# Slots of four samples instead of two in a streaming matmul with residual

## The chip, the cores and the metric

The kernel runs on one core of one Trainium2 chip. The metric is the device time of one execution in microseconds (us). The kernel before takes 327.6 us, the median of three runs (327.56 to 327.68).

## The reference

There are 128 samples, each a matrix of 128 channels by 1024 time steps in float32 (512 KB). Each sample has a subject number from 0 to 7, which picks one of eight 128 by 128 weight matrices. The output is the sample plus the product of its weights and itself:

```python
def reference(x, itok_B_0_7, L0_cond_weights):
    ...
        w = weights[subjects]
        out = jnp.einsum('bct,bcd->bdt', x, w)
        return out
    x = x + _L0_cond_ref(x, itok_B_0_7, L0_cond_weights)
    return x
```

So 67.1 MB are read, 67.1 MB are written, and between the two stand 128 products of a 128x128 matrix with a 128x1024 matrix.

## The kernel before, in words

The samples stay in SBUF in slots. A slot holds `G` = 2 samples side by side: in each of the 128 partitions (one for each channel) it has 2 x 1024 values, 8 KB without a gap. There are `SLOTS` = 23 slots, thus room for 46 samples, and `NT` = 128 / 2 = 64 turns of the loops over slots. Turn `i` uses slot `i % SLOTS`. The sum is written back over the sample in the slot, and the slot is stored from there.

Each engine has its own program, written out by hand in the order in which it runs; semaphores tie them together.

- SP issues the loads (L114 to L124), one DMA of 512 KB for each sample. From the second use of a slot on, it first waits until the store of the slot's last content has landed (L117). The load reads the sample in HBM as 32 runs of 16 KB (`ROWS` = 4 rows of 4 KB); each run goes to four partitions.
- POOL copies the weights of a sample's subject from `w_all`, which holds all eight matrices, into one of four small buffers (L142). It waits first for the load of `w_all` (L126), and for each sample until the product of four samples ago is done (L141).
- PE waits once for each slot until all loads of the slot have landed (L129), then for each sample for its weights (L144) and a free PSUM buffer (L146), and does two matmuls of 512 columns (L148). The profile shows each as two instructions, so there are four for a sample.
- DVE adds product and sample into the slot (L158), one instruction for each sample.
- ACT waits until all samples of the slot are added (L161) and issues one store for the whole slot, 1 MB (L162 to L167). From SBUF it reads one run for each partition, 8 KB; in HBM these go to two rows of 4 KB in two samples.
- At the end SP waits for the stores of the last `SLOTS` turns (L170, L171).

Loads and stores are issued through the function `transfer`, so that the profile puts both under L49. They use two DMA queues: q1 is SP's with the loads, q10 is ACT's with the stores, the load of `w_all` and that of the subject numbers. Each DMA ends with 16 writes of a semaphore, one for each DMA engine that took part.

Of the kernel before, what the change touches and what calls it, by code (L numbers as in the profile page):

```python
# [1 line left out]

# [4 lines left out]

F32 = mybir.dt.float32
I32 = mybir.dt.int32
ALU = mybir.AluOpType


G = 2

N = 512  # L30

SLOTS = 23

W_SLOTS = 4
P_SLOTS = 4
DMA = 16

ROWS = 4
QUEUES = {mybir.EngineType.SP: "qSPDynamicHW", mybir.EngineType.Activation: "qActDynamicHW"}


def transfer(nc, engine, out, in_):

    later, nc._always_lower_symbolic_ap = nc._always_lower_symbolic_ap, False
    ins, outs = engine.lower_ap_dma(in_), engine.lower_ap_dma(out)
    nc._always_lower_symbolic_ap = later
    return engine.add_instruction(  # L49
        mybir.InstDMACopy(  # L50
            name=nc.get_next_instruction_name(),
            engine=engine.engine,
            ins=ins,
            outs=outs,
            mode="Copy",
            cce_op=ALU.bypass,
            queue=QUEUES[engine.engine],
        )
    )


@with_exitstack
def kernel(
    ctx: ExitStack,
    tc: tile.TileContext,
    x: bass.AP,
    subjects: bass.AP,
    weights: bass.AP,
    out: bass.AP,
):  # L70
    nc = tc.nc
    B, C, T = x.shape
    S, _, D = weights.shape
    NT = B // G

    def sbuf(name, *shape, dtype=F32):
        return ctx.enter_context(nc.sbuf_tensor(name, list(shape), dtype)).ap()

    given, near, wrap, index = (
        sbuf(name, 1, B, dtype=I32) for name in ("given", "near", "wrap", "index")  # L80
    )
    w_all = sbuf("w_all", C, S, D)
    ws = [sbuf(f"w{i}", C, 1, D) for i in range(W_SLOTS)]
    xs = [sbuf(f"x{i}", C, G, T) for i in range(SLOTS)]
    ps = [
        ctx.enter_context(nc.psum_tensor(f"ps{i}", [D, T], F32)).ap() for i in range(P_SLOTS)
    ]

    s_given = tc.alloc_semaphore("s_given")
    s_wall = tc.alloc_semaphore("s_wall")  # L90
    s_index = tc.alloc_semaphore("s_index")
    s_copied = tc.alloc_semaphore("s_copied")
    s_product = tc.alloc_semaphore("s_product")
    s_added = tc.alloc_semaphore("s_added")
    s_load = [tc.alloc_semaphore(f"s_load{i}") for i in range(SLOTS)]
    s_store = [tc.alloc_semaphore(f"s_store{i}") for i in range(SLOTS)]

    with tc.tile_critical():  # L98

        nc.scalar.dma_start(given, subjects.rearrange("(o b) -> o b", o=1)).then_inc(s_given, DMA)  # L100
        nc.scalar.dma_start(w_all, weights.rearrange("s c d -> c s d")).then_inc(s_wall, DMA)

        nc.vector.wait_ge(s_given, DMA)
        nc.vector.tensor_scalar(near, given, -S, S - 1, ALU.max, ALU.min).then_inc(s_index, 1)  # L106
        nc.vector.wait_ge(s_index, 1)
        nc.vector.tensor_scalar(wrap, near, 0, S, ALU.is_lt, ALU.mult).then_inc(s_index, 1)  # L108
        nc.vector.wait_ge(s_index, 2)
        nc.vector.tensor_tensor(index, near, wrap, ALU.add).then_inc(s_index, 1)  # L110
        nc.gpsimd.wait_ge(s_index, 3)


        for i in range(NT):  # L114
            k, turn = i % SLOTS, i // SLOTS
            if turn:
                nc.sync.wait_ge(s_store[k], DMA * turn)  # L117
            for g in range(G):
                transfer(
                    nc,  # L120
                    nc.sync,
                    xs[k][:, g, :],
                    x[i * G + g].rearrange("(a r) t -> a (r t)", r=ROWS),
                ).then_inc(s_load[k], DMA)  # L124

        nc.gpsimd.wait_ge(s_wall, DMA)  # L126
        for i in range(NT):
            k, turn = i % SLOTS, i // SLOTS
            nc.tensor.wait_ge(s_load[k], DMA * G * (turn + 1))  # L129
            for g in range(G):  # L130
                b = i * G + g
                s = nc.values_load(  # L132
                    index[0:1, b : b + 1],
                    engines=[mybir.EngineType.Pool],
                    min_val=0,
                    max_val=S - 1,
                    skip_runtime_bounds_check_because="the index is clamped on the chip above",
                )
                w, p = ws[b % W_SLOTS], ps[b % P_SLOTS]
                if b >= W_SLOTS:  # L140
                    nc.gpsimd.wait_ge(s_product, b - W_SLOTS + 1)  # L141
                nc.gpsimd.tensor_copy(w, w_all[:, bass.ds(s, 1), :]).then_inc(s_copied, 1)  # L142

                nc.tensor.wait_ge(s_copied, b + 1)  # L144
                if b >= P_SLOTS:
                    nc.tensor.wait_ge(s_added, b - P_SLOTS + 1)  # L146
                for t in range(0, T, N):
                    mm = nc.tensor.matmul(  # L148
                        p[:, t : t + N],
                        w[:, 0, :],  # L150
                        xs[k][:, g, t : t + N],
                        start=True,
                        stop=True,
                    )
                mm.then_inc(s_product, 1)

                nc.vector.wait_ge(s_product, b + 1)
                nc.vector.tensor_tensor(xs[k][:, g, :], p, xs[k][:, g, :], ALU.add).then_inc(  # L158
                    s_added, 1
                )  # L160
            nc.scalar.wait_ge(s_added, (i + 1) * G)  # L161
            transfer(  # L162
                nc,
                nc.scalar,
                out[i * G : (i + 1) * G].rearrange("g d t -> d g t"),
                xs[k].rearrange("d (o g) t -> d o (g t)", o=1),
            ).then_inc(s_store[k], DMA)  # L167


        for i in range(NT - SLOTS, NT):  # L170
            nc.sync.wait_ge(s_store[i % SLOTS], DMA * (i // SLOTS + 1))  # L171


# [1 line left out]
_INS = ["x", "itok_B_0_7", "L0_cond_weights"]  # L175
_OUTS = [((128, 128, 1024), "float32")]


# [20 lines left out]
```

## Time and profile before

| what | value |
|---|---|
| median of three runs | 327.6 us |
| the profiled execution | 328.1 us |
| its span, first to last instruction | 326.3 us |
| PE busy | 237.0 us (73%) |
| DVE busy | 157.5 us (48%) |
| POOL busy | 37.8 us (12%) |
| DMA moved | 134.86 MB, mean 413 GB/s over the span |
| a matmul of 512 columns, mean | 616 ns, 592 ns at full clock |
| an add of one sample | 1225 ns |
| a load, issue to landing, median | 21.4 us |
| a store, issue to landing, median | 42.2 us |

The profile is of one execution. Its slices cut the span into 40 equal parts of 8.2 us; a digit is a busy share in tenths. For each DMA queue the page gives packets, MB and the time that the packets took, as a share of the time of 16 DMA engines. The same table can be had for a window of the span. A wait is told as "who waited <- for what: us in total, times, longest us". The chain of work is followed back from the last instruction, and its lines give start, duration and what ran. SPq and ACTq are the instruction queues of SP and ACT, which issue DMAs. PEclk is the clock that TensorE was granted, in tenths.

### The profile page before, as it was taken

What the parts mean: (1) busy time and instruction counts of PE and PEld (TensorE: products, weight loads), DVE (VectorE), ACT (ScalarE), POOL (GpSimd) and SP (SyncE); (2) the same over time, 40 slices, a digit from 0 to 9 for tenths busy, and PEclk for the clock granted to TensorE, in tenths of its full rate; (3) what the DMA queues carried; (4) which work ended last, traced back from release to release, by engine and by line L of the source; (5) the groups of instructions that cost most, each with busy time, mean ns of one, the idle gap of its engine ahead of it and who ended that gap; (6) DMA issues with size and microseconds to landing.
All of it is one profiled execution on the core that took longest, in us unless ns stands there. A gap on an engine that the chain in (4) does not pass through costs nothing.

```text
span 326.3 us, 1928 instructions
## 1 busy us (share of the span) xinstructions
PE 237.0 (73%) x512; PEld 97.1 (30%) x512; DVE 157.5 (48%) x131; POOL 37.8 (12%) x132
## 2 busy tenths in 40 slices
PE   0499999999999888999989887775979877000000
PEld 0144444444443333333333332231433332000000
DVE  0067766776677556556566554545445536000000
POOL 0111111111111111111111111111111100000000
PEclk9999999999999999999999999999798979755555
DMA  7999999999999999999999999999999999999993
GB/s 268 407 416 422 420 425 419 425 426 423 429 425 421 427 422 428 419 427 424 419 426 420 428 422 434 417 429 423 425 429 426 427 420 425 427 426 427 428 424 164
DMA packets 16411, 134.86 MB, mean 413 GB/s; under 512 B 3089, under 2 KB 4114, under 8 KB 4114
## 3 DMA queue, kind: packets, MB, share of 16 engines
q10 hardware_dynamic: 10258, 67.64, 49.6%
q1 hardware_dynamic: 6144, 67.12, 49.1%
q8 instruction: 4, 0.07, 0.1%
q14 instruction: 5, 0.04, 0.0%
HBM read 67.63 MB, written 67.11 MB: 413 GB/s over the span
## 4 chain that ended last, share of the span: by engine, by line
DMA 37%; another core or an unknown queue 22%; PE 17%; SPq 7%; DVE 1%; issue 1%; POOLq 0%; ACTq 0%; POOL 0%
DMA out_dram<-x 29%; PE ps L148 17%; SPq L49 7%; DMA x<-in_x_dram 5%; DMA w_all<-in_L_cond_weights_dram 3%; DVE x L158 1%; POOLq L132 0%; ACTq L100 0%; POOLq L142 0%; ACTq L195 0%; POOL w L142 0%; POOLq L126 0%; SPq L98 0%
## 5 line engine op out<-in xcount | busy, mean ns | idle before, releaser
L148 PE MATMUL ps<-x,w 128*128 128x512 f32 x512 | 237.0, 616 | 38.8 <-DMA x<-in_x_dram 26.2
L158 DVE TENSOR_TENSOR x<-ps,x 128x1024 f32<-128x1024 f32 x128 | 156.8, 1225 | 117.3 <-PE ps L148 117.3
L148 PEld LDWEIGHTS ps<-x,w 128*128 128x128 f32 x512 | 97.1, 195 | 177.8 <-issue 122.4
L142 POOL COPY w<-w_all 128x128 f32 x128 | 37.6, 294 | 230.6 <-PE ps L148 218.4
L106 DVE TENSOR_SCALAR near<-given 1x128 int32<-1x128 int32 x1 | 0.2, 215 | 2.2 <-DMA given<-in_itok_B_dram 2.2
L110 DVE CUSTOM_DVE_ANT_0 index<-near,wrap 1x256 uint16<-1x256 uint16 x1 | 0.3, 280 | 0.0
L108 DVE TENSOR_SCALAR wrap<-near 1x128 int32<-1x128 int32 x1 | 0.2, 216 | 0.0
L186 POOL MEMSET const-float32-0.0<- 128x1 f32 x1 | 0.1, 98 | 0.2 <-issue 0.2
L186 POOL MEMSET const-bfloat16-1.0<- 128x1 bf16 x1 | 0.1, 101 | 0.0
L186 POOL MEMSET const-uint8-127<- 128x1 uint8 x1 | 0.1, 101 | 0.0
L186 POOL MEMSET const-float32-1.0<- 128x1 f32 x1 | 0.1, 98 | 0.0
## 6 DMA issues: line engine op xcount, KB each, us to landing
x<-in_x_dram SPq DMA_DIRECT2D x128, 512.0 KB, 21.4
out_dram<-x ACTq DMA_DIRECT2D x64, 1024.0 KB, 42.2
w_all<-in_L_cond_weights_dram ACTq DMA_DIRECT2D x1, 512.0 KB, 10.0
given<-in_itok_B_dram ACTq DMA_DIRECT2D x1, 0.5 KB
```

The costliest lines, as they stand in the source:

```text
L49: return engine.add_instruction(mybir.InstDMACopy(name=nc.get_next_instruction_name(), engine=engine.engine, ins=ins, outs=outs, mode="Cop ...
L106: nc.vector.tensor_scalar(near, given, -S, S - 1, ALU.max, ALU.min).then_inc(s_index, 1)
L108: nc.vector.tensor_scalar(wrap, near, 0, S, ALU.is_lt, ALU.mult).then_inc(s_index, 1)
L110: nc.vector.tensor_tensor(index, near, wrap, ALU.add).then_inc(s_index, 1)
L142: nc.gpsimd.tensor_copy(w, w_all[:, bass.ds(s, 1), :]).then_inc(s_copied, 1)
L148: mm = nc.tensor.matmul(p[:, t : t + N], w[:, 0, :], xs[k][:, g, t : t + N], start=True, stop=True,)
L158: nc.vector.tensor_tensor(xs[k][:, g, :], p, xs[k][:, g, :], ALU.add).then_inc(s_added, 1)
L186: nc = _bacc.Bacc("TRN2", target_bir_lowering=False, num_devices=1)
```

## The change

Two constants change. A slot holds four samples, and there are 12 slots for 23, room for 48 samples instead of 46. The loops over slots make 32 turns.

```diff
-G = 2
+G = 4

 N = 512

-SLOTS = 23
+SLOTS = 12
```

All that follows from them: PE's wait at L129 is for four loads; ACT's wait at L161 is for four adds; a store carries 2 MB and reads, from each partition, one run of 16 KB, which goes to four rows of 4 KB in four samples; SP waits at L117 for a store of four samples before it issues four loads; and the last loop waits for 12 stores. The loads themselves, the weights, the matmuls and the adds stay as they are, in the same order on each engine; ACT has 32 stores to issue for 64.

## The prediction, made before the changed kernel was run

> **What bounds the kernel now.** I read the page first: slices, queues, groups.
>
> ```profile
> DMA  7999999999999999999999999999999999999993
> GB/s 268 407 416 422 420 425 419 425 426 423 429 425 421 427 422 428 419 427 424 419 426 420 428 422 434 417 429 423 425 429 426 427 420 425 427 426 427 428 424 164
> ...
> q10 hardware_dynamic: 10258, 67.64, 49.6%
> q1 hardware_dynamic: 6144, 67.12, 49.1%
> ```
>
> The 16 DMA engines are full from the second slice to the last but one, while PE is busy 73% and DVE 48%. Only two things can move the time: what the same 134 MB cost in engine time, and idle time of the engines at the two ends. q1 carries the loads, q10 the stores. Counts explain themselves: 128 loads x (32 runs of 16 KB + 16 semaphore writes) = 6144; 64 stores x (128 runs of 8 KB + 16) = 9216, and the rest of q10 is w_all.
>
> Next, how the queues share the engines where both have a backlog (60 to 110 us), then the loads alone (12 to 24) and the stores alone (290 to 320).
>
> ```profile
> DMA packets 2339, 21.22 MB, mean 424 GB/s; under 512 B 523, under 2 KB 523, under 8 KB 523
> ...
> q1 hardware_dynamic: 1167, 12.65, 60.1%
> q10 hardware_dynamic: 1169, 8.53, 40.8%
> ...
> x<-in_x_dram SPq DMA_DIRECT2D x24, 512.0 KB, 32.5
> ```
> ```profile
> DMA packets 452, 4.88 MB, mean 407 GB/s; under 512 B 154, under 2 KB 154, under 8 KB 154
> ...
> q1 hardware_dynamic: 452, 4.88, 100.3%
> ```
> ```profile
> DMA packets 1751, 12.76 MB, mean 425 GB/s; under 512 B 194, under 2 KB 194, under 8 KB 194
> ```
>
> See 1167 against 1169: the queues take turns packet by packet, the 4-byte semaphore writes counting as packets. Per engine, three loads are 3 x (2 + 1) = 9 turns for 96 KB and one store is 8 + 1 = 9 turns for 64 KB, so loads get 1.5 times the bytes (12.65 / 8.53 = 1.48). Loads run ahead, stores pile up. The queue's own waits and the end of the chain show what this leads to.
>
> ```profile
> SPq L49 <- DMA out_dram<-x: 116.5, 28, 5.1
> SPq L171 <- DMA out_dram<-x: 59.4, 11, 35.2
> ```
> ```profile
> 216.57 47.05 DMA out_dram<-x
> ...
> 264.15 7.88 DMA x<-in_x_dram
> 272.03 0.04 issue
> 272.07 3.71 PE ps L148 x8
> 275.79 0.02 issue
> 275.81 1.23 DVE x L158
> ```
>
> The last load lands at 272.0, the last add ends at 277.0, and for 47 us more the engines write stores that have piled up. Thus the compute of the last slot costs nothing today.
>
> **What the Trainium skill says.** "DMA: Bandwidth & Descriptors", section "Queues, rings and completion order": each DMA engine goes round-robin between queue rows, at packet granularity. The trace agrees (1167 to 1169), with one run of 8 or 16 KB a packet. Same page, "Why a DMA increments its semaphore by 16 and not by 1": each engine's last descriptor is the semaphore write; the 16 small packets per DMA agree. Same page, "Where 436 GB/s comes from": the ceiling is 435 GB/s; 424 here leaves 2.6% for any packet saving. "TensorE: Matmul & The Clock Gate", "What's actually happening": the clock falls to half after an idle window of about 3.4 us. Here PE halves for 3.4 us at 229.8, 243.5 and 264.0, each after a wait of some 2.4 to 4 us for a load.
>
> **The change part by part.**
>
> *Store runs of 16 KB.* The trace's packet records have medians of 311 ns (8 KB store) and 616 ns (16 KB load beside stores). 4096 pairs become 4096 single packets: 4096 x (622 - 616) / 16 engines = -1.5 us. Bounds: from the shares of 60 to 110 (16 engines x 50 us = 800 us; of the packets 8/9 and 2/3 carry data), 40.8% x 800 / 1039 = 314 and 60.1% x 800 / 778 = 618, so -2.6; above, 640 ns as when loads run alone (100.3% x 192 us / 301), +4.6. I take -1.5.
>
> *Half the stores.* 512 semaphore packets fewer x 9 ns / 16 = -0.3 us. ACT issues 32 DMAs for 64, SP still 128; neither issue is late today.
>
> *Slots of four, loads.* PE's L129 waits for four loads. Slot 0: the fourth load lands at 10.3, but PE starts at 12.65, held by POOL's copy from w_all: cost 0, and if w_all came earlier, under 3 us. Behind PE's wait stand the slot's matmuls, then POOL's copies and DVE.
>
> *First store.* ACT waits for four adds, two more x 1.72 us (add to add at full clock) = 3.4 us later, issue at 23.8. The first store's packets came 4.3 us after its issue (20.4, 24.7), so now 28.1. Loads fill those 3.4 us (15 are outstanding: 24 x 32.5 / 50), at 407 for 424 GB/s: +0.1 us.
>
> *The turns.* A 2 MB store is still 9 turns per engine, now for 128 KB, against 96 KB of loads. Loads get 0.75 of the stores' bytes. A sample is 0.524 MB, so 424 GB/s = 0.809 samples/us: loads 0.347 (2.88 us each), stores 0.462 (2.16 us). At 28.1 some 17.9 samples have landed (15 by 24.4, then one per 1.28 us) and none is stored. The gap shrinks by 0.116 samples/us. PE, at 1.72 us a sample, catches up with the loads at about 76 us. A store then needs 8.4 us from landing to issue, 4.3 us to its first packet and 8.6 us to drain; with a slot of 9.9 us (4.19 MB / 424 GB/s) this holds about 9 samples between load and store. (17.9 - 9) / 0.116 = 77 us: from about 105 us there is no pile, and PE, ACT and stores follow the loads. SP's slot waits vanish: 9 + 15 outstanding is far below 48. Each period of 9.9 us then has loads alone for 1.3 us at 407: 0.05 us x 21 periods = +1.1 us.
>
> *The end.* Call the last landing T. The slot before landed at T - 9.9; its store, issued at T - 1.5, is written after T, behind the rest (0.8 us) of the one before it: engines busy to T + 0.8 + 4.9 = T + 5.7. The last slot: four samples. Today two take 277.04 - 272.03 = 5.0 us, four 5.0 + 2 x 1.72 = 8.4, and issue to first packet is 1.3 us on free engines (first load: issue 0.95, packets 2.3): T + 9.8. Idle 4.0 us. PE now waits some 3 us per slot, so a halved window in the last slot is about even: 3.4 us at half clock cost 1.7 us. I take idle 4.9; bounds 2.4 (last slots closer together) and 8 (two windows). Then 4.9 us for the 2 MB, as long as its bytes take anyway. What covered this today was the pile.
>
> Sum: -1.5 - 0.3 + 0.1 + 1.1 + 4.9 = +4.3 us. The profiled execution took 328.1 (span 326.3 and 1.8 around it), so 332.4; the median of the runs shown is 327.6, 0.5 lower: 331.9 us.
>
> **The rivals.**
>
> *The pile stays (not slower).* If a semaphore write takes no turn, stores and loads with equal runs share equally, the gap of 17.9 samples remains, and at T there are 22 us of stores to hide 9.8 us. For: both have 16 KB runs. Against: the packet counts of 60 to 110; without those turns the bytes would stand 2 to 1. It decides at a gap of 11.8 samples at T (7.8 to cover 9.8 us, and the last four). Over some 283 us this is a shrinking of 0.0216 per us, loads at 0.95 of the stores' bytes. Then -1.5 - 0.3 + 0.1: 327.6 - 1.7 = 325.9.
>
> *The runs stay 8 KB.* If a run were split at the 4 KB rows of out into today's pieces, a store has 17 turns, loads get 1.4 times the bytes, the pile stays: -0.3 and +0.1, 327.4. Against: loads make 16 KB packets with 4 KB pieces on the other side.
>
> *Long packets cost more.* At 640 ns a packet, +4.6 in place of -1.5, beside the exposed end: 338. Against: stores alone reach 425, loads alone 407, so stores are the easier side.
>
> **How the numbers follow.** Measurement tells about 0.2% (0.7 us) from no change. Exposed end 0.66 (its own range 329 to 336, some 0.03 of it under 328.3); pile stays 0.21; runs stay 8 KB 0.06; costly packets 0.07. Slower 0.70, same 0.09 (runs stay 8 KB, edges of the others), faster 0.21. The range, 325.8 to 336, reaches the hidden end's time and leaves out about half of that case and the costly packets.
>
> **What would show it.** Right: q10 with some 5,600 packets; equal packet counts in 60 to 100 us with MB at 3 to 4; no SP wait for stores before L171; last load at about 314 of a span of 330.5 rather than 272; PE, DVE and one store at the chain's end; a hole of 4 to 6 us in the DMA share before the last 5 us; store packets near 616 ns. Wrong: loads that land before 300, a long stretch of stores alone, SP still waiting for slots in mid-kernel, or store packets away from 616.

## The result and the profile after

The changed kernel takes 332.7 us (median of 12 runs, 328.9 to 335.6) against 327.9 us (327.4 to 328.4) of the kernel before: 1.0106 times as long, 95% interval 1.008 to 1.0133. The ratio leaves out runs more than 1.5% above the fastest of their kernel, here three of the changed one; the medians of all twelve stand at 1.0147. In a later comparison the ratio was 1.016 (1.0143 to 1.0177). The profiled execution has a span of 331.2 us, 4.9 more than before, and the last packet of its stores ends 5.2 us later (324.2 and 329.4).

The page of the changed kernel, DMA share and rate in 40 slices of 8.3 us, then the two queues:

```profile
DMA  7999999999999999999999999999999999999555
GB/s 275 406 410 429 417 432 421 431 417 437 416 437 416 420 429 423 427 419 429 421 433 416 425 427 427 421 421 433 419 429 421 430 421 419 429 423 431 232 253 253
...
q1 hardware_dynamic: 6144, 67.12, 48.5%
q10 hardware_dynamic: 5650, 67.64, 48.3%
```

Up to the 37th slice the rate is that of before, some 425 GB/s. The last three slices, 25 us, move 232 to 253 GB/s. All of the loss is there: by 306.4 us the kernel before had moved 128.6 MB and the changed one 128.8. q10 has 5650 packets for 10258: the store runs are 16 KB, as the change says.

How the queues share the engines while both have a backlog, 26 to 48 us of the changed kernel:

```profile
q10 hardware_dynamic: 359, 5.36, 57.3%
q1 hardware_dynamic: 365, 4.03, 43.5%
```

Equal packets again, 359 and 365, but now the loads get 0.75 of the stores' bytes (4.03 / 5.36), where before they got 1.48 times as much. The stores no longer pile up: a store lands in a median of 13.6 us (42.2 before), and SP never waits for a slot in the loop. Its waits for stores, and those of PE for loads, in the changed kernel ("us in total, times, longest us"):

```profile
SPq L171 <- DMA out_dram<-x: 53.5, 6, 10.5
```
```profile
PE ps L148 <- DMA x<-in_x_dram: 72.6, 25, 10.2
```

The 116.5 us of slot waits at L49 are gone; PE now waits for loads 72.6 us in all. Before, it was 26.2:

```profile
PE ps L148 <- DMA x<-in_x_dram: 26.2, 34, 2.5
```

The end of the chain, and the last 31 us of the DMA engines in 40 slices of 0.78 us, both of the changed kernel, and then the last 26 us of the kernel before:

```profile
274.96 39.66 DMA x<-in_x_dram
314.62 0.04 issue
314.66 7.15 PE ps L148 x16
321.81 0.02 issue
321.84 1.22 DVE x L158
```
```profile
DMA  9989989998999431000077899770000799779400
GB/s 486 402 381 465 486 360 402 465 465 359 423 486 423 190 148 63 21 21 0 0 338 338 338 550 465 338 338 0 0 0 0 338 486 529 338 338 507 169 0 0
```
```profile
DMA  9999999999999999999999999999999643100000
```

The last load lands at 314.6 (272.0 before). Two holes stand in the second view: one at 310 to 316, while the last load's straggling packets and the last but one slot's adds are waited for, and one at 321 to 324, while the last slot's four samples are computed. Then the last store has the engines to itself. Summed from the packet records, the mean engine is idle for 8.1 us from 15 us before the last landing of a load to the last packet of a store; before it was 2.0. Below this is called the idle time at the end.

### The profile page after: what moved, and what is told of

The parts are those of the page before. It is cut to its first block, busy times and chain, and to the rows that moved or that the text cites. A ratio compares the mean times of both kernels' runs of the same rounds, so it can differ in the third digit from the quotient of the medians.

```text
span 331.2 us, 1890 instructions
## 1 busy us (share of the span) xinstructions
PE 249.2 (75%) x512; PEld 103.9 (31%) x512; DVE 157.5 (48%) x131; POOL 37.8 (11%) x132
## 3 DMA queue, kind: packets, MB, share of 16 engines
q10 hardware_dynamic: 5650, 67.64, 48.3%
## 4 chain that ended last, share of the span: by engine, by line
SPq 81%; DMA 12%; PE 2%; issue 2%; DVE 0%
SPq L49 81%; DMA x<-in_x_dram 12%; PE ps L148 2%; DVE x L158 0%; SPq L195 0%; SPq L98 0%
## 5 line engine op out<-in xcount | busy, mean ns | idle before, releaser
L148 PE MATMUL ps<-x,w 128*128 128x512 f32 x512 | 249.2, 646 | 72.6 <-DMA x<-in_x_dram 72.6
L148 PEld LDWEIGHTS ps<-x,w 128*128 128x128 f32 x512 | 103.9, 208 | 217.0 <-issue 124.4
## 6 DMA issues: line engine op xcount, KB each, us to landing
out_dram<-x ACTq DMA_DIRECT2D x32, 2048.0 KB, 13.6
```

What stands on the lines that cost most here:

```text
L148: mm = nc.tensor.matmul(p[:, t : t + N], w[:, 0, :], xs[k][:, g, t : t + N], start=True, stop=True,)
```

## The experiments

The theory under test (turns): each DMA engine gives the load queue and the store queue one packet each in turn, semaphore writes included; the changed store moves 128 KB an engine in nine turns, the loads 96 KB, so the pile of stores melts, and the last slot's compute and store lie open. The rivals: slots of four cost by themselves, because PE and ACT wait for four (slot theory); or the long store packets cost engine time (packet theory).

**Slots of four, stored in two halves.** The slot waits stay, the store's turns go back.

```diff
+            for h in range(0, G, 2):
...
-                out[i * G : (i + 1) * G].rearrange("g d t -> d g t"),
-                xs[k].rearrange("d (o g) t -> d o (g t)", o=1),
+                    out[i * G + h : i * G + h + 2].rearrange("g d t -> d g t"),
+                    xs[k][:, h : h + 2, :].rearrange("d (o g) t -> d o (g t)", o=1),
...
```

(The waits for a slot's stores count both.)

> Slots of four as in the change, but each slot is stored by two DMAs of 1 MB with runs of 8 KB, as before. Turns theory (stores of 9 turns for 128 KB an engine drain faster than loads, no pile is left, the end of the last slot lies open): a store is again 9 turns for 64 KB, loads get 1.5 times the bytes, the pile stays, so 327.9 us as the kernel before (327.4 to 328.3), last load at about 270 us. Slot theory (waiting for four loads and four adds costs by itself): 331 to 332, as the changed kernel. Packet theory (the long packets cost engine time): 327.9, but with stores alone at the same rate as the changed kernel's loads.

Measured: 327.9 us, ratio to before 0.9998 (0.999 to 1.0007). Its window of 60 to 110 us, and the chain's end:

```profile
q1 hardware_dynamic: 1153, 12.62, 59.8%
q10 hardware_dynamic: 1159, 8.45, 40.5%
```

```profile
262.30 10.70 DMA x<-in_x_dram
273.01 0.04 issue
273.05 8.53 PE ps L148 x16
281.58 0.03 issue
281.61 1.23 DVE x L158
```

The loads have 1.49 times the stores' bytes again, and the last load lands at 273.0. PE still handles the last four samples after one wait, 8.53 us of matmuls, but it is over at 283 of 326 us; the pile of stores covers it. The slot theory falls: with the pile, slots of four cost nothing.

**The changed kernel with 32 KB load runs.** `ROWS = 8` for 4.

> The changed kernel with loads of 32 KB runs (16 for each sample in place of 32). A load is then 1 data packet and 1 semaphore write an engine, 2 turns for 32 KB or 16 KB a turn, against a store's 128 KB in 9 turns, 14.2 KB a turn. Turns theory: loads get 1.125 times the stores' bytes, the pile stays, the open end goes, and what is left of the change is its saving of packets: 326 us (325.3 to 326.8), faster than the kernel before, equal packet counts of both queues while both have a backlog. Slot theory and packet theory: 331 or more, since slots, stores and store packets are those of the changed kernel.

Measured: 350.9 us, ratio 1.0642 (1.0587 to 1.0698), far from the 326 expected. Two windows of this kernel, 60 to 110 us and, with the loads all but alone, 5 to 30 us:

```profile
q1 hardware_dynamic: 681, 11.27, 54.0%
q10 hardware_dynamic: 680, 9.83, 46.6%
```
```profile
DMA packets 1144, 6.68 MB, mean 267 GB/s; under 512 B 192, under 2 KB 952, under 8 KB 952
...
q1 hardware_dynamic: 368, 6.29, 100.5%
```

The turns went as computed (681 to 680, loads 1.15 times the stores' bytes) and the pile came back: a store lands in 36.3 us. But a 32 KB load packet takes 1371 ns in the mean, where two of 16 KB take 1246. The mean hides two cases: beside stores, at 60 to 110 us, it is 1247 ns, as two short ones; with the loads alone, at 12 to 24 us, it is 2084 ns for two of 641, and loads move 267 GB/s in place of 407. The load packets sum to 16 us more an engine, 11 of them in the first 31 us. At the end the engines finish one after another, from 337.7 to 347.5 us. So this run speaks for the turns and says nothing on the end's price. Why the longer read is slow alone, and why the engines drift apart, was not followed.

**Only the last slot by single samples.** The last four loads have a semaphore each, PE waits for each, and four stores of 512 KB follow.

```diff
+                if i == NT - 1:
+                    nc.tensor.wait_ge(s_lastload[g], DMA)
...
+                if i == NT - 1:
+                    nc.scalar.wait_ge(s_added, b + 1)
+                    transfer(nc, nc.scalar, out[b], xs[k][:, g, :]).then_inc(s_laststore[g], DMA)
```

> The changed kernel, but the last slot alone is handled sample by sample: PE waits for each of its four loads, and four stores of 512 KB (runs of 4 KB) carry it out. Turns theory: the pile is gone as in the changed kernel (last load at about 314 us), but the last sample is ready some 3.4 us after its landing and its store needs only 1.2 us, while the slot before is still being written; of the open end of 5 us some 4 go: 327.5 us (326.8 to 328.5). Slot theory: 31 of 32 slots still wait for four, 331. Packet theory: 31 of 32 stores are still long, 331.

> The changed kernel once more beside the others, on the same chip: 329 to 335 us, median near 332, all theories alike.

Measured: 328.3 us, ratio 1.0017 (1.0006 to 1.0029), against 332.9 us, 1.016 (1.0143 to 1.0177), for the changed kernel beside it. So 4.6 us of the 5.0 us between the medians of the changed kernel and the one before go with the handling of one slot in 32: the slot theory fails here too, since the other 31 still wait for four. The packet theory falls as well: 31 long stores are still there. The last load lands at 314.2, as in the changed kernel; the idle time at the end falls to 2.7 us. Its DMA engines at 300 to 326 us:

```profile
DMA  9999999999999998430009999999989999999000
```

The second profile of the changed kernel had 4.8 us of idle time for the 8.1 of the first, and a span of 328.0 for 331.2: between these two, the end makes the whole difference.

**The kernel before with 8 KB load runs.** `ROWS = 2` for 4, slots and stores as before. It makes the pile melt without slots of four.

> The kernel before (slots of two, stores of 1 MB) with loads of 8 KB runs in place of 16 KB. A load is then 4 data packets and 1 semaphore write, 5 turns for 32 KB or 6.4 KB a turn, against a store's 64 KB in 9 turns, 7.1 KB a turn. Turns theory: loads get 0.9 of the stores' bytes (equal packet counts), the pile melts away by the end, the last slot of two lies open by some 1 to 2 us, and 4096 more packets cost 1.5 us: 331 us (329.8 to 332). If a semaphore write takes no turn, the shares are equal, the pile of the start stays, and only the packets cost: 329.4.

Measured: 330.4 us, ratio 1.0076 (1.0059 to 1.0093). Its window of 60 to 110 us:

```profile
q10 hardware_dynamic: 1532, 11.24, 53.6%
q1 hardware_dynamic: 1522, 9.98, 47.7%
```

Equal packets, loads at 0.89 of the stores' bytes (0.90 computed). The stores' landing falls from 20.7 us for the one issued at 92 us to 9.0 for the one at 308, the last load lands at 317.7, and the idle time at the end is 5.1 us. The slot theory has no word for this: two samples a slot, no pile, and the time goes up. Of its 2.6 us the load packets hold 1.1 (160.27 for 159.14 us, the sum of all packets divided by 16). The idle time rose by 3.1; the two together are more than the 2.6, and what makes up for the rest was not traced.

**Half of the matmuls.** The second of a sample's two matmuls is left out, so the upper half of each product stays at the zeros that DVE writes to PSUM at the start.

```diff
+        for p in ps:
+            nc.vector.memset(p, 0.0).then_inc(s_zero, 1)
...
-                for t in range(0, T, N):
+                for t in range(0, N, N):
```

> The changed kernel without the second of the two matmuls of each sample (the upper half of the product is left at the zeros written to PSUM at the start). PE then needs 0.86 us a sample, and the adds at 1.27 us set the pace of a slot. Turns theory: the last slot's store starts 7.3 us after its last landing in place of 9.8, and half-clock windows cost less: 328 us (327.2 to 329.2) and less scatter, 3 to 4 below the changed kernel. Packet theory: no difference, 331 to 332, since all DMAs are the same.

> The kernel before without the second of the two matmuls of each sample, the counterpart of the run before. All theories: PE is hidden by the pile of stores, 327.9 us (327.4 to 328.4).

Measured: 331.0 us (330.3 to 331.6) from the changed kernel, ratio to before 1.0101 (1.0083 to 1.0118), and 327.1 us, 0.998 (0.9971 to 0.9989), from the one before. Both lie outside their ranges: the first above, the second a little below. The first is about 2 us under the changed kernel's medians, not 3 to 4, and even these 2 are not shown: that kernel's own runs go from 328.9 to 335.6, and its first ratio, 1.0106, is nearly the same. So this pair decides nothing between the theories. The profile tells why shorter compute did not help more. The issue of the last store came 6.7 us after the last landing for 8.5. But the store before it also moved up, from 0.2 us after the last landing to 2.4 us before it, and so less of it was left to cover the last slot: the idle time at the end is 5.7 us, between the 8.1 and the 4.8 of the changed kernel.

**PE waits for single samples everywhere.** One semaphore for each load; stores are still 2 MB.

```diff
-            nc.tensor.wait_ge(s_load[k], DMA * G * (turn + 1))
...
+                nc.tensor.wait_ge(s_load[k * G + g], DMA * (turn + 1))
```

> The changed kernel with a semaphore for each load, so that PE starts a sample when that sample has landed; the stores are still 2 MB and wait for four adds. Turns theory: no pile either, but the last store is issued some 3.4 us after the last landing in place of 8.4; the store before it starts as much earlier, so the idle time at the end falls by 3 to 4 us and not by 5: 329 us (328 to 330). If waiting for whole slots cost along the way and not only at the end, 328 or less; if only the 2 MB store counts, 332.

Measured: 329.2 us (328.9 to 329.4), ratio 1.004 (1.0025 to 1.0056), as computed. The last store is issued 3.3 us after the last landing, the one before 6.6 us before it, and 4.3 us of idle time stay. TensorE's mean clock is 0.993 for 0.919, and the runs scatter by 0.5 us (four runs) for 6.8 (twelve). That the half-clock windows make the scatter fits this, but the run changes waits and clock together.

**Slots of three.** `G = 3`, `SLOTS = 15`, the last turn with two samples. Nine turns now move 96 KB on both sides.

> Slots of three samples (15 slots, the last turn holds two): a store is 1.5 MB in runs of 12 KB, still 8 data packets and 1 semaphore write an engine, 9 turns for 96 KB, exactly what three loads move in 9 turns. Turns theory: equal bytes, above the deciding 0.95; the 16 samples that are ahead when the stores begin stay ahead, the end is hidden, and a part of the packet saving is left: 327.0 us (326.5 to 327.9), last load at about 290 us. Slot theory (waiting for more samples costs by itself): half way between before and after, 330.

Measured: 327.6 us, ratio 0.9995 (0.9987 to 1.0004). Its window of 60 to 110 us:

```profile
q10 hardware_dynamic: 969, 10.68, 50.5%
q1 hardware_dynamic: 962, 10.52, 49.9%
```

Equal bytes; a store lands in 29 us, and the last slot is hidden. The last load lands at 307, not at 290: the pile holds, but smaller than I took it. Waiting for three samples costs nothing; the saved packets do not show either.

**Stores held back, so that a pile is there at the end.** Slots and DMAs are those of the changed kernel; ACT waits longer before it issues a store (`LAG` is 3). The first form and the second, which releases the held stores one slot earlier, follow. In both PE's waits are the changed kernel's; a third form is the second with PE's waits for single samples.

```diff
-            nc.scalar.wait_ge(s_added, (i + 1) * G)
+            nc.scalar.wait_ge(s_added, B if i == NT - 1 else min(i + 1 + LAG, NT - 1) * G)
```
```diff
+            nc.scalar.wait_ge(s_added, max(i + 1, min(i + 1 + LAG, NT - 2)) * G)
```

> The changed kernel, slots, loads and stores as they are, but ACT issues each store only when the slot three turns later has been added; the stores that this holds back are all released before the last slot, whose own store waits for nothing else. So a pile of four stores is there when the last load lands. Turns theory: it hides the last slot, the tail's idle time falls from 5 to 8 us to about 2, and the time to 327.3 us (326.5 to 328.2), at or under the kernel before. Slot theory and packet theory: 331 or more, since all waits of PE and all DMAs are those of the changed kernel.

> The lagged stores, but the held stores are released one slot earlier, when the last but two of the slots has been added. In the first form the loads ran out some 5 us before the release, and the DMA engines stood at 16 to 144 GB/s in a hole of 4 us. Turns theory: four stores are then queued about 11 us before the last landing, the hole closes, nothing else changes, and the saved packets show: 326.6 us (325.9 to 327.5), under the kernel before. If the gain of packets is only apparent, 328 as the first form.

> The same release, and PE waiting for each sample by itself: its waits are short, so TensorE should keep its full clock to the end (0.99 in the run with fine waits alone) and the times should scatter less. Turns theory: the end was hidden already, so the same 326.6 us (325.9 to 327.5). Slot theory, if waiting for four costs something besides the end: under 326.

Measured: 328.2 us, 1.0021 (1.0009 to 1.0033); 327.9 us, 1.0006 (0.9997 to 1.0014); 328.2 us, 1.001 (1.0004 to 1.0017). The first form at 285 to 310 us, and the second at 285 to 326 us, in 40 slices each:

```profile
GB/s 419 419 419 419 446 419 419 419 446 420 419 472 419 446 419 446 446 341 210 105 52 26 105 393 367 393 472 367 419 419 419 420 419 498 446 446 472 498 419 419
```
```profile
DMA  9999999999999999999999999999999999831000
```

Holding stores back brings the changed kernel to within 0.2% of the kernel before, and to within 0.1% in the second form, with nothing else in the program touched, and the idle time at the end is 2.2, 1.9 and 2.6 us: the pile is what was missing. The hole at 296 to 299 is the hold itself, and the second form closes it. No form beats the kernel before: 326.6 was expected of the second and third, 327.9 and 328.2 were measured. Nor do the fine waits make the times scatter less here: 0.8 us with them and without.

## Why the prediction was right

- **What bounds the kernel, and the turns:** as told. Loads at 0.75 of the stores' bytes were computed and measured; across the runs the computed shares 1.5, 1.125, 1.0, 0.9 and 0.75 stand beside 1.48, 1.15, 0.985, 0.89 and 0.75, always with equal packet counts. The deciding point of 0.95 lies between slots of three (no loss) and the 8 KB loads (loss); it was not narrowed further.
- **When the pile melts:** too late. PE was to catch up with the loads at about 76 us; its first wait for them began at 47.0. From about 105 us there was to be no pile; the store issued at 82.8 us already landed in 13.4 us. The failing term compared single samples, while PE starts a slot only when all four are there. That is a part of the gap and not all of it: with waits for single samples PE first waits at 57.5. Another part is the lead of the loads, 16 samples at 28.1 us where 17.9 were computed. It did not matter for the end.
- **Packets, -1.5 and -0.3:** the store packets sum to 158.00 us an engine for 159.48, so -1.48, the small packets of q10 hold 0.24 us less, and the median 16 KB store packet took 616 ns. Yet the three kernels that have long stores and a hidden end (slots of three, stores held back and released, the same with fine waits) are not faster than before. The saving exists in the packet records and not in the time. Where stores were held back and released, the load packets took back half of it: 159.99 us for 159.14.
- **Loads alone, +0.1 and +1.1:** oversized. The load packets sum to 159.42 us for 159.14, +0.3.
- **The end, +4.9:** last load at 314.6 (about 314 computed), last store issued 8.5 us after it (8.4). The idle time at the end rose by 6.2 us in the first profile and by 2.8 in the second, on both sides of the 4.9. The first has a half-clock window in the last but one slot (16 matmuls in 8.82 us for 7.13), which moved its store from the computed 1.5 us before the last landing to 0.2 us after it. The first profile's sum is -1.7 + 0.3 + 6.2 = 4.8 us, beside the measured 5.2 between the last packets; the other 0.4 was not traced.
- **The sum, +4.3:** the medians moved by 4.8 us, and by the ratio of 1.0106 it is 3.5. The steps were right; that the sum came so near is partly luck. The loads' term was 0.9 us too large, and the end, the largest term, differs by more than 3 us between two profiles of one kernel.
- **The rivals:** the pile did not stay, the runs are 16 KB, the packets are not dear.

## What to carry to other kernels

Where two DMA queues compete, count packets for each, semaphore writes among them, and multiply by their length: in these runs that ratio told, at each of five settings, which stream got how much. A stream of stores that lagged cost nothing here and hid the last slot's compute; a change that lets the stores keep up moves that compute to the end of the span. Before enlarging a DMA, look whether a smaller last tile or a held store is needed to cover the end.

## What the runs showed beyond this

- Load runs of 32 KB are slower than those of 16 KB where the loads are alone (267 for 407 GB/s), but not beside stores at 60 to 110 us (1247 ns a packet, for two of 618 in the kernel before).
- In most kernels with a hidden end one DMA engine finishes last by itself: 324.2 us, the other fifteen at 320.5 to 322.5, before, and 324.2 against 319.7 to 321.8 with slots of three. The fifteen gained some 0.8 us from longer packets and the one did not. That the one sets the time, and so swallows the saving, fits; why it lags was not tested. With half of the matmuls left out, and so fewer instructions to fetch (two 16 KB instruction packets for four), the kernel before got 0.2% faster, and its last engine ended at 323.2 us. That the fetches make the one engine late is not shown.
- In the changed kernel TensorE's clock fell to half after eleven of PE's waits for a slot, of 2.2 to 4.7 us, and not after five others of 2.7 to 3.1 us. In the kernel before, the waits ahead of its three half-clock windows were 2.5, 2.2 and 2.4 us by PE's own record, where the prediction has 2.4 to 4; so the clock also fell after waits shorter than the 3.4 us told there. With waits for single samples, none above 1.2 us after the start, it stayed at full speed nearly throughout (0.993).
